# Layer 0 of a spectral attention kernel: where the next image batch's sums, loads and spectra stand, and what GpSimd does behind attention's products

## The chip, the cores and the metric

One core of a Trainium2 chip. The time is the device time of one execution of the program in microseconds (us); below, the median of several executions. A profiled execution gives the trace: what each engine did at each moment. Engines are named as the profile names them: PE is the matmul engine and PEld its weight loads, DVE is VectorE, ACT is ScalarE, POOL is GpSimd, SP is the queue of SyncE that issues transfers.

## The reference, cut to what matters

The input x has shape (4, 32, 128, 128): 4 batches of 32 images. Layer 0 normalises x by groups, runs a spectral attention block on each batch and adds it to x; layer 1 (token attention and experts) follows and isn't touched by the change.

```python
x = x + _L0_conv_ref(_gn(x), ...)
# within _L0_conv_ref, for each batch:
xn = _inorm(xa, norm1_w, norm1_b)              # every image to mean 0, variance 1
k, q, v = (_fno_layer(xn, ...) for K, Q, V)    # spectral convolutions to 32 heads
scores = einsum('bntk,bnsk->bnts', qf, kf) / sqrt(Hs * Ws)   # image against image, per head
p_attn = softmax(scores);  av = einsum('bnts,bnsk->bntk', p_attn, vf)
p = _fno_layer(av, Pcw, Psw, H, W)
a = _inorm(p + xa, attn_w, attn_b);  an = _inorm(a, norm2_w, norm2_b)
m = _fno_layer(an, m0cw, m0sw, H, W, inner_norm=True, act=True)    # gelu
m = _fno_layer(m, m1cw, m1sw, H, W, inner_norm=True, act=False)
out = _inorm(m, mon_w, mon_b) + a
```

## The kernel before, in words

Everything is computed in frequency space. Layer 0 is a Python loop `for b in range(B)` (line 702) over the four batches. The trace calls a batch's 32 images together "image b" below. What b + 1 needs at its start is prepared inside the body of b. In program order, a pass of the loop is:

- `load(b + 1)` (lines 122 to 127, called at 707): four transfers of 512 KB, two on SP's queue and two on ACT's, into the second of two x buffers.
- The head weights: `cm` (718), `cd` (720), `cp` (721), `bd` (726), which are made of the attention weights `ph` and needed by the skip products `sk` (757).
- The value loop over `x0` in five steps of four (766 to 803): a broadcast of the spectra (`xb`, 773, on SP), a copy to PSUM (`xw`, ACT, 782), products with the value weights (`u`, 788 on POOL, 790 on DVE), and matmuls into `po` (793) with the weights `pr`.
- Back to images (813, `inverse` at 267), statistics, the first spectra of q (`spectra(0, q)`, 937), the chain of scale factors `v0`, `r0`, `hq`, `hs0`, `hb` (938 to 949), then `back` (288) with the gelu (956 to 966).
- `logarithms()` (972) puts the logarithm table back on ACT; `image_sums(b + 1)` (320 to 393, called at 974): squares of x (326), matmuls that sum rows (330), then a chain of small operations on DVE with two inverse deviations, each a logarithm and an exponential on ACT (`inv_std`, 203).
- `stats("gl")`, `spectra(1, gl)` (982), `spectra_of_images(b + 1)` (418 to 459, called at 984), and the second scale chain `v1`, `vc`, `r1`, `rm`, `c2`, `cq` (985 to 1007).
- `attention_weights(b + 1)` (489 to 595, called at 1009). It copies rows to PSUM (`xp`, 501), and for each of 17 column frequencies `yy` makes two products, `pa` on DVE (534) and `pb` on POOL for even `yy` and on DVE for odd (533 to 536), which PE multiplies into `sp` (540, 542). Then come `spt` (544), the logits `sc` in two halves one after the other (549 to 558), softmax (562 to 579), and two transfers by way of HBM that give `pr` (587, 592).
- The end (1010 to 1031): ACT scales g (1014), POOL adds it to the residue in four pieces (`xr`, 1021), `back` runs again and DVE adds its result (1025), and SP stores x1 (1031).

The order of instructions on each engine isn't written out: within layer 0 the framework's scheduler orders them at build time. What is earlier in the program has priority, and what is ready and finds its buffer free can be taken ahead of its place. Buffers are shared by tag. In PSUM the tags "wide" (two buffers of two banks), "a" and "b" (two of one bank each) take all eight banks: `rows8`, `s12` and the small sums of `image_sums` are "wide", and so are `xp`, `so`, `sc`, `y1` of `back`, and `xw`. In SBUF the tag "pr" has six buffers, shared by the squares, `u`, `sod`, `pa`, `pb`, `spt`, `ex` and `ph`; "pk" and "pk_sq" have one each, shared by `image_sums` and `stats`. Layer 1 has an order written out by hand and starts when layer 0 is done with PE.

Of the kernel before, what the change touches and what calls it, by code (L numbers as in the profile page):

```python
# [7 lines left out]
F32 = mybir.dt.float32  # L8
AF = mybir.ActivationFunctionType
ALU = mybir.AluOpType  # L10
# [98 lines left out]
def layer0(  # L109
# [11 lines left out]

    def load(b):
        xt = images.tile([P, T, C], F32, name=f"x_{b}", tag="x")
        for g in range(0, T, GI):
            eng = nc.sync if g % 16 == 0 else nc.scalar
            eng.dma_start(out=xt[:, g : g + GI], in_=x[b, g : g + GI].rearrange("t w c -> w t c"))
        return xt
# [50 lines left out]
    grp, small = (p.__enter__() for p in work)  # L178
    pools += work

    flip = [0]
# [70 lines left out]

    def forward(images, c1, c2, take, change):


        n = c1.shape[1]
        z = grp.tile([P, GI, 192], F32, name="z", tag="z")
        first_step(images, z)
        change(z)
        for k in range(0, GI, 4):  # L260
            px = ps.tile([P, 4, n], F32, name="px", tag="b")
            for j in range(4):
                nc.tensor.matmul(px[:, j], z[:, k + j, :P], c1, start=True, stop=False)
                nc.tensor.matmul(px[:, j], z[:, k + j, 64:], c2, start=False, stop=True)
            take(k, px)
# [44 lines left out]

    def sums(name, matrix, src):

        m = ps.tile(list(src.shape), F32, name=name, tag="wide")
        nc.tensor.matmul(m, matrix, src, start=True, stop=True)
        return m

    def one(name, n=1):
        return small.tile([P, n], F32, name=name, tag=name)

    def image_sums(b, xt):  # L320


        rows8 = ps.tile([64, 4, C], F32, name="rows8", tag="wide")
        for g in GROUPS:
# [13 lines left out]
        nc.scalar.copy(ev, rows8)  # L338
        s12 = ps.tile([P, 2, 512], F32, name="s12", tag="wide")[:, :, :T]
        for j in range(4):  # L340
            for k in range(2):
                r = slice(32 * k, 32 * k + 8)
                nc.tensor.matmul(s12[:, k, j::4], ev[r, j], ident[r, r], start=True, stop=True)
        sv = small.tile([P, 2, T], F32, name="sv", tag="pk_sq")
        nc.vector.tensor_copy(sv, s12)

        tot = one("tot", 2)
        nc.vector.tensor_reduce(tot, sv, AX.X, ALU.add)
        mg = sums("mg", group, tot)
        gm = one("gm")  # L350
# [11 lines left out]
        by_group = small.tile([P, 2, 32], F32, name="by_group", tag="by_group")  # L362
        nc.vector.tensor_copy(by_group, sums("bg", ones, both))
        n = 1 + 2 * KY
        colg = small.tile([P, 2, n], F32, name="colg", tag="colg")
        nc.vector.tensor_scalar(colg[:, 0], cols1[:, :n], gr, None, ALU.mult)
        nc.vector.tensor_scalar(colg[:, 1], cols2[:, :n], gr, None, ALU.mult)
        m128 = one("m128")
        nc.vector.tensor_scalar(m128, gm, 128.0, None, ALU.mult)

# [14 lines left out]
        nc.vector.tensor_scalar(y12, y12, 1.0 / NPIX, None, ALU.mult)  # L385
        my = sums("my", ones, y12)
        ym, yv = per_image("ym"), per_image("yv")
# [4 lines left out]
        ysc = scalars(ALU.mult, "n1_s", yr, par[:, N1W : N1W + 1])  # L392
        return by_group, colg, m128, ysc

# [23 lines left out]
    def spectra_of_images(b, xt, normed):  # L418


        _, colg, m128, ysc = normed
        n = 1 + 2 * KY
        xx = modes.tile([P, T, n], F32, name=f"xx_{b}", tag="xx")
        xd = dram.tile([T, 2, KX, KY], F32, name=f"xd_{b}")
        for g in GROUPS:

# [5 lines left out]

            def less_mean(z):
                nc.vector.tensor_scalar(z[:, :, 0], z[:, :, 0], m128, None, ALU.subtract)
                nc.vector.tensor_scalar(z[:, :, P], z[:, :, P], m128, None, ALU.add)

            forward([xt[:, g + t] for t in range(GI)], colg[:, 0], colg[:, 1], scaled, less_mean)

# [49 lines left out]

    def attention_weights(b, front):

# [36 lines left out]
        for yy in range(KA):  # L527
# [3 lines left out]
            for k, t in enumerate((pa, pb)):  # L531
                other = (xm[:, yy] if k else xe[:, yy, :T]).unsqueeze(2).to_broadcast(tt)
                if k == 0 or yy % 2 == 1:
                    nc.vector.tensor_tensor(t, steps(row, [1, T], [1, nd]), other, ALU.mult)
                else:
                    nc.gpsimd.tensor_tensor(t, steps(xe[:, yy], [1, T], [1, nd]), other, ALU.mult)
            turn = dict(start=yy < 2, stop=yy >= KA - 2)
# [10 lines left out]
        sc = ps.tile(nn, F32, name="sc", tag="wide")  # L548
        for h in range(2):
            i = slice(half * h, half * h + half)  # L550
            o = sc[32 * h : 32 * h + 32]
            nc.tensor.matmul(o, qk, sod[:, i], start=True, stop=False)
            nc.tensor.matmul(o[:, :, 1:nd], both_plus, spt[:, 0, i], start=False, stop=False)
            first = spt.rearrange("p r t d -> p (r t d)")[:, (half * h + nd) * half + half - 2 :]
            nc.tensor.matmul(
                o[:, :, nd:], plus_minus, steps(first, [half, half], [half - 1, half - 1]), start=False, stop=False
            )
            nc.tensor.matmul(o[:, :, 0], both_plus[: 2 * NH], spt0[:, i], start=False, stop=True)


# [22 lines left out]
        for k in range(2):  # L583
# [10 lines left out]
            )  # L594
        return ph, pr

# [50 lines left out]
    big, late = (p.__enter__() for p in (pools[-1], right[-1]))  # L647
    weights = attention_weights(0, front)

# [42 lines left out]

    pv = const.tile([2 * NH, 1], F32, name="pv")
    nc.sync.dma_start(out=pv[:NH], in_=heads[:, 2:3])
    nc.sync.dma_start(out=pv[NH:], in_=heads[:, 2:3])
    psw2 = const.tile([2 * NH, 1], F32, name="psw2")
    nc.sync.dma_start(out=psw2[:NH], in_=heads[:, 3:4])
    nc.sync.dma_start(out=psw2[NH:], in_=heads[:, 3:4])
    nc.vector.tensor_mul(pv, pv, psw2)


    for b in range(B):
        xt = loaded
        by_group, _, _, ysc = normed
        xd = front[2]
        if b + 1 < B:
            loaded = load(b + 1)

        ph, pr = weights

        cp = per_image("cp")
        sel = scalars(ALU.mult, "sel", same, ysc)
        for h in range(2):
            r = slice(32 * h, 32 * h + 32)
            cm = ps.tile([P, T, 16], F32, name="cm", tag="a")
            nc.tensor.matmul(cm, pv[r].to_broadcast([NH, P]), ph[r], start=True, stop=True)
            cd = grp.tile([P, T, 16], F32, name="cd", tag="v", bufs=3)
            nc.vector.tensor_tensor(cd, cm, sel.unsqueeze(2).to_broadcast([P, T, 16]), ALU.mult)  # L720
            nc.vector.tensor_reduce(
                cp[:, 16 * h : 16 * h + 16], cd.rearrange("p s t -> p t s"), AX.X, ALU.add
            )
        nc.vector.tensor_add(cp, cp, same)
        bd = small.tile([P, 4, T], F32, name="bd", tag="bd")
        nc.vector.tensor_tensor(
            bd,
            block.unsqueeze(2).to_broadcast([P, 4, T]),
            cp.unsqueeze(1).to_broadcast([P, 4, T]),
            ALU.mult,  # L730
        )
        q = big.tile([P, T, C], F32, name=f"q_{b}", tag="q")
# [33 lines left out]
        for x0 in range(0, KX, NK):  # L766
# [3 lines left out]
            for i in range(4):  # L770
                xb = late.tile([P, 2, NK * KY], F32, name="xb", tag="xb")[:, :, :m]
                for r in range(2):
                    nc.sync.dma_start(
                        out=xb[:, r],
                        in_=xd[8 * i : 8 * i + 8, r, x0 : x0 + nk]
                        .rearrange("s x y -> s (x y)")
                        .unsqueeze(1)
                        .to_broadcast([8, 16, m]),
                    )
# [20 lines left out]
                if i % 2 and at_c < C:  # L800
                    skips(at_c)
                    at_c += 16
            nc.scalar.copy(rs[:, x0 : x0 + nk].rearrange("p x y -> p (x y)"), po)
        if b + 1 == B:
            for p in reversed(right):
                p.__exit__(None, None, None)
# [141 lines left out]
        nc.vector.tensor_mul(dq, dq, hs0)  # L948
        nc.vector.tensor_tensor(hb, hb, dq, ALU.add)
        gl = big.tile([P, T, C], F32, name=f"g_{b}", tag="y")  # L950
        st = grp.tile([P, T, 6], F32, name="st", tag="st")
# [20 lines left out]
        logarithms()  # L972
        if b + 1 < B:
            normed = image_sums(b + 1, loaded)
        else:
            first((ps, images))
# [5 lines left out]
        spec, sq = spectra(1, gl)  # L982
        if b + 1 < B:
            front = spectra_of_images(b + 1, loaded, normed)
        v1 = weighed("v1", sq, squares, layers[1][2])
# [22 lines left out]
        if b + 1 < B:  # L1008
            weights = attention_weights(b + 1, front)
        for a in HALVES:  # L1010
            groups = [slice(16 * a + g, 16 * a + g + GI) for g in (0, GI)]
            for i in groups:
                for t in range(i.start, i.stop):
# [6 lines left out]
                    )  # L1020
                nc.gpsimd.tensor_tensor(xr[:, i], xr[:, i], gl[:, i], ALU.add)

# [638 lines left out]
```

## Time and profile before

| what | value |
|---|---|
| median of 3 runs | 3184.4 us (3181.8 to 3186.39) |
| the profiled execution, its own time | 3176.48 us |
| its span, first to last instruction | 3174.4 us |
| busy share of the span: PE, DVE, ACT, POOL | 92%, 71%, 73%, 65% |
| mean granted PE clock | 0.954 |
| first `po` matmul of images 0, 1, 2, 3 | 107.33, 362.84, 623.00, 882.33 us |
| first matmul of layer 1's attention (1461) | about 1088 us |

Two successive images are 255 to 260 us apart. The profile's page lists busy time by engine, the chain of waits that ended last, and groups of instructions by line; the trace gives each instruction's start, its duration, and, where its engine had been idle, for how long and what ended that. "PEclk" is the granted share of PE's full clock.

### The profile page before, as it was taken

The page shows a single profiled execution, that of the slowest core. Times are in us where ns is not written, and L with a number is a line of the kernel's source. Part 1 is how long each engine was busy: PE and PEld are TensorE (multiplying, and loading weights), DVE is VectorE, ACT ScalarE, POOL GpSimd, SP SyncE. Part 2 cuts the span into 40 slices and gives each one's busy share as a digit, 9 for nine tenths or more (in the row PEclk, how much of TensorE's full clock was granted, in tenths as well). Part 3 has the DMA queues.
Part 4 walks back from the last instruction along what each step waited for, and adds up shares of the span by engine and source line. Part 5 has one row for each costly group of instructions (what it writes and reads, how often), then busy time and mean ns, then how long its engine had stood idle before and what let it go on. Part 6 is the DMA issues. An engine that isn't in the chain of part 4 may idle for free.

```text
span 3174.4 us, 52863 instructions
## 1 busy us (share of the span) xinstructions
PE 2911.8 (92%) x19530; PEld 1437.6 (45%) x19530; DVE 2257.4 (71%) x5054; ACT 2318.2 (73%) x3142; POOL 2053.0 (65%) x1819
## 2 busy tenths in 40 slices
PE   7888889798888789999999999999999999999997
PEld 4366366355446444444344444443444444444443
DVE  5776676667578557777666868866778776777887
ACT  2444343354354589998999999998999999999992
POOL 1621440350270388878888797889878889888773
PEclk8898898799798799999999999999999999999998
DMA  6401310220130201010111010021010011101000
GB/s 139 120 10 30 107 39 22 72 82 1 38 124 1 66 23 31 9 29 7 31 37 24 14 24 14 7 46 29 17 37 1 14 37 24 37 1 31 14 14 14
DMA packets 152306, 112.74 MB, mean 36 GB/s; under 512 B 36878, under 2 KB 140657, under 8 KB 151441
## 3 DMA queue, kind: packets, MB, share of 16 engines
q1 hardware_dynamic: 136209, 103.61, 12.3%
q10 hardware_dynamic: 15840, 5.77, 0.8%
q8 instruction: 154, 2.52, 0.3%
q14 instruction: 103, 0.84, 0.1%
HBM read 68.37 MB, written 20.00 MB: 28 GB/s over the span
## 4 chain that ended last, share of the span: by engine, by line
PE 62%; POOL 12%; ACT 9%; DVE 8%; issue 6%; DMA 2%; SPq 0%; POOLq 0%; DVEq 0%; ACTq 0%
PE d L1461 19%; PE po L1480 11%; PE px L1367 6%; ACT r L1511 5%; PE po L793 4%; PE n L1461 3%; POOL e L1520 3%; POOL e L1519 3%; PE pz L248 2%; PE four L308 2%; ACT e L1527 2%; PE px L886 2%; POOL kx L1126 1%; PE sk L757 1%; DVE r L1516 1%
## 5 line engine op out<-in xcount | busy, mean ns | idle before, releaser
L1516 DVE TENSOR_TENSOR r<-n,r 128x1024 f32<-128x1024 f32 (+1 forms) x1056 | 962.0, 953 | 478.3 <-PE n L1461 393.4
L1519 POOL TENSOR_TENSOR e<-r 128x512 f32<-128x512 f32 x528 | 673.0, 1275 | 268.7 <-DVE r L1516 268.1
L1511 ACT ACTIVATE r<-d 128x1024 f32<-128x1024 f32 (+1 forms) x1056 | 792.8, 802 | 68.8 <-PE n L1461 59.0
L1523 ACT ACTIVATE r<-r 128x1536 f32<-128x1536 f32 x528 | 783.6, 1484 | 16.8
L1520 POOL TENSOR_TENSOR e<-e,r 128x512 f32<-128x512 f32 x528 | 671.2, 1271 | 41.4
L1461 PE MATMUL d<-qe,ke 32*128 32x512 f32 (+3 forms) x2304 | 606.3, 602 | 39.8 <-ACT r L1511 36.5
L1480 PE MATMUL po<-e,kx 128*128 128x512 f32 (+3 forms) x1152 | 594.5, 605 | 15.7 <-POOL e L1532 15.7
L1461 PE MATMUL n<-qe,ke 32*128 32x512 f32 (+3 forms) x2304 | 606.7, 602 | 0.0
L1461 PE MATMUL n<-qf,kf 32*128 32x512 f32 (+3 forms) x2304 | 552.7, 554 | 0.0
L1461 PE MATMUL d<-qf,kf 32*128 32x512 f32 (+3 forms) x2304 | 550.3, 553 | 0.0
L1371 DVE SCALAR_TENSOR_TENSOR xc<-px,wgt,xc 128x128 f32<-128x128 f32 x1024 | 358.4, 351 | 43.0 <-PE px L1367 10.5
L1527 ACT ACTIVATE e<-e 128x512 f32<-128x512 f32 x528 | 325.8, 617 | 65.9 <-POOL e L1520 65.1
L1480 PEld LDWEIGHTS po<-e,kx 128*128 128x128 f32 x1152 | 175.5, 188 | 393.0 <-issue 308.5
L1461 PEld LDWEIGHTS d<-qe,ke 32*128 32x128 f32 x2304 | 176.5, 183 | 359.6 <-ACT r L1511 339.8
L788 POOL TENSOR_TENSOR u<-xb,gb 128x858 f32<-128x858 f32 (+1 forms) x120 | 233.5, 1968 | 156.6 <-PE po L793 110.4
L1461 PEld LDWEIGHTS d<-qf,kf 32*128 32x128 f32 x2304 | 220.4, 186 | 176.2 <-issue 164.1
L1367 PE MATMUL px<-we,x2t 128*128 128x512 f32 x512 | 265.9, 605 | 6.9 <-DVE xc L1371 5.9
L790 DVE TENSOR_TENSOR u<-xw,gb 128x858 f32<-128x858 f32 (+1 forms) x200 | 206.9, 1086 | 58.3 <-PE po L793 51.8
L1461 PEld LDWEIGHTS n<-qf,kf 32*128 32x128 f32 x2304 | 228.7, 185 | 18.9 <-issue 11.1
L900 POOL TENSOR_TENSOR spec<-part,part 128x512 f32<-128x512 f32 x16 | 24.8, 1552 | 323.7 <-DVE part L897 80.3
L793 PE MATMUL po<-u,pr 128*32 128x429 f32 (+1 forms) x1280 | 194.0, 551 | 26.3 <-DVE u L790 14.4
L1461 PEld LDWEIGHTS n<-qe,ke 32*128 32x128 f32 x2304 | 177.8, 183 | 9.2 <-DVE r L1516 0.8
(395 smaller groups left out, 3760.5 us busy)
## 6 DMA issues: line engine op xcount, KB each, us to landing
xb<-xd SPq DMA_DIRECT2D x128, 214.5 KB
xc<-x SPq DMA_DIRECT2D x29, 512.0 KB
x<-x SPq DMA_DIRECT2D x16, 512.0 KB
qf<-qe SPq DMA_DIRECT2D x64, 128.0 KB
out<-xc SPq DMA_DIRECT2D x15, 512.0 KB
xb<-xd SPq DMA_DIRECT2D x32, 198.0 KB
gb<-gd SPq DMA_DIRECT2D x4, 1056.0 KB
x<-in_x SPq DMA_DIRECT2D x8, 512.0 KB
```

The lines of the kernel that those rows point to most:

```text
L788: nc.gpsimd.tensor_tensor(u, xb, gk, ALU.mult)
L793: nc.tensor.matmul(po[32 * j : 32 * j + 32], pr[:, i, k], u[:, r], start=i == 0 and k == 0, stop=i == 3 and k == 1,)
L1367: nc.tensor.matmul(px, x2t[:, k * P : (k + 1) * P], we[:, e0 : e0 + 4], start=True, stop=True)
L1371: nc.vector.scalar_tensor_tensor(xc[:, k], px[:, e], wgt[:, k, e0 + e : e0 + e + 1], xc[:, k], ALU.mult, ALU.add)
L1461: nc.tensor.matmul(o, k, q, start=turn == 0 or g > 0, stop=turn == 1 or g > 0)
L1480: nc.tensor.matmul(sums[c, h][:, q0 : q0 + c1 - c0], kx[:, jb], e[:, c0:c1], start=jb == 0, stop=is_last and q0 > 2 * P, skip_group_check= ...
L1511: nc.scalar.activation(r[:, g], d, AF.Ln, scale=1.0 / DSCALE)
L1516: nc.vector.tensor_tensor(r[:, g], part, r[:, g], ALU.mult)
L1519: nc.gpsimd.tensor_tensor(e, r[:, 1], r[:, 2], ALU.add)
L1520: nc.gpsimd.tensor_tensor(e, e, r[:, 0], ALU.add)
L1523: nc.scalar.activation(r, r, AF.Exp, scale=-1.0)
L1527: nc.scalar.activation(e, e, AF.Exp)
```

## The change

It touches layer 0 alone, in these places:

1. **Products.** `pb` goes to DVE where `yy % 3 == 2` (5 of 17) and to POOL otherwise (12 of 17); before, 8 and 9. The four POOL additions of line 1021 get an order edge behind the last POOL product.
2. **Logits.** The two halves of `sc` are issued in turn, matmul by matmul, instead of one half after the other.
3. **Head weights.** `cm`, `cd`, `cp`, `bd` move from the head of the pass into the end of `attention_weights`, ahead of the second `back`.
4. **Image sums.** `image_sums(b + 1)` moves from behind the gelu to ahead of it; its PSUM tiles go from "wide" to "a" and "b".
5. **Spectra.** In `spectra_of_images` the first step of group g + 1 is issued ahead of the second step of group g; the mean's removal is one DVE addition instead of two operations. The whole function moves behind the second scale chain.
6. **Loads.** `load(b + 1)` moves into the value loop, after its second `x0` step, all four transfers on SP with an order edge behind that step's last broadcast. The loads of `pv` and `psw2` in the prologue come before the first `attention_weights`.

```diff
@@ load
-            eng = nc.sync if g % 16 == 0 else nc.scalar
+            eng = nc.sync if behind is not None or g % 16 == 0 else nc.scalar
...
+            if behind is not None:
+                tc.add_manual_dep(d.ins, behind.ins.name, ...NoSync..., reason="order")
@@ image_sums
-        rows8 = ps.tile([64, 4, C], F32, name="rows8", tag="wide")
+        rows8 = ps.tile([64, 4, C], F32, name="rows8", tag="a")
...
-        s12 = ps.tile([P, 2, 512], F32, name="s12", tag="wide")[:, :, :T]
+        s12 = [ps.tile([P, T], F32, name=f"s{t}", tag=t) for t in "ab"]
...
-        mg = sums("mg", group, tot)
+        mg = sums("mg", group, tot, "a")
@@ spectra_of_images
-        for g in GROUPS:
+        steps = []
+        for g in (*GROUPS, None):
+            if g is not None:
+                z = grp.tile([P, GI, 192], F32, name="z", tag="z")
+                first_step([xt[:, g + t] for t in range(GI)], z)
+                nc.vector.tensor_tensor(
+                    z[:, :, ::P], z[:, :, ::P], shift.unsqueeze(1).to_broadcast([P, GI, 2]), ALU.add
+                )
+                steps.append((g, z))
+                if g == 0:
+                    continue
+            g, z = steps.pop(0)
...
-            def less_mean(z):
-                nc.vector.tensor_scalar(z[:, :, 0], z[:, :, 0], m128, None, ALU.subtract)
-                nc.vector.tensor_scalar(z[:, :, P], z[:, :, P], m128, None, ALU.add)
@@ attention_weights
-                if k == 0 or yy % 2 == 1:
+                if k == 0 or yy % 3 == 2:
...
-                    nc.gpsimd.tensor_tensor(t, steps(xe[:, yy], [1, T], [1, nd]), other, ALU.mult)
+                    last_product = nc.gpsimd.tensor_tensor(t, steps(xe[:, yy], [1, T], [1, nd]), other, ALU.mult)
...
-        for h in range(2):
-            i = slice(half * h, half * h + half)
-            o = sc[32 * h : 32 * h + 32]
+        halves = [(sc[32 * h : 32 * h + 32], slice(half * h, half * h + half)) for h in range(2)]
+        for o, i in halves:
             nc.tensor.matmul(o, qk, sod[:, i], start=True, stop=False)
+        for o, i in halves:
             nc.tensor.matmul(o[:, :, 1:nd], both_plus, spt[:, 0, i], start=False, stop=False)
...
-        return ph, pr
+        cp = per_image("cp")
+        sel = scalars(ALU.mult, "sel", same, ysc)
...
+        return pr, bd, last_product
@@ loop over b
-        if b + 1 < B:
-            loaded = load(b + 1)
...
             nc.scalar.copy(rs[:, x0 : x0 + nk].rearrange("p x y -> p (x y)"), po)
+            if x0 == NK and b + 1 < B:
+                loaded = load(b + 1, broadcast)
...
         nc.vector.tensor_tensor(hb, hb, dq, ALU.add)
+        if b + 1 < B:
+            normed = image_sums(b + 1, loaded)
...
         logarithms()
-        if b + 1 < B:
-            normed = image_sums(b + 1, loaded)
-        else:
+        if b + 1 == B:
             first((ps, images))
...
         spec, sq = spectra(1, gl)
-        if b + 1 < B:
-            front = spectra_of_images(b + 1, loaded, normed)
...
         if b + 1 < B:
-            weights = attention_weights(b + 1, front)
+            front = spectra_of_images(b + 1, loaded, normed)
+            weights = attention_weights(b + 1, front, normed[3])
...
-                nc.gpsimd.tensor_tensor(xr[:, i], xr[:, i], gl[:, i], ALU.add)
+                added = nc.gpsimd.tensor_tensor(xr[:, i], xr[:, i], gl[:, i], ALU.add)
+                if b + 1 < B:
+                    behind(added, weights[2])
```

## The prediction, made before the result was known

> **What bounds the kernel now.** I read the page first. The profiled execution took 3176.5 us, its span 3174.4. In its 40 slices PE is at 9 tenths from the sixteenth on (layer 1 begins at 1088 us), and before that between 7 and 9 tenths, at a clock of 7 to 9 tenths. The change touches only the first third, so I cut one period of that, from image 1's value loop to image 2's, into stages and asked for busy times and clock in each.
>
> ```profile
> core 0: us, PE busy (x) PEld busy (x) DVE busy (x) ACT busy (x) POOL busy (x), PEclk, DMA share, GB/s
> 362.80:431.40 68.60, 65.21 (x640) 30.20 (x640) 50.38 (x51) 38.53 (x84) 54.09 (x28) 0.96 0.45 134
> 431.40:471.50 40.10, 38.56 (x430) 34.17 (x430) 27.39 (x94) 12.86 (x24) 1.27 (x1) 0.96 0.01 2
> 471.50:484.00 12.50, 4.71 (x66) 4.35 (x66) 11.67 (x39) 1.45 (x4) 2.17 (x1) 0.58 0.00 1
> 484.00:504.90 20.90, 20.87 (x114) 9.59 (x116) 16.97 (x66) 18.17 (x40) 0.00 (x0) 0.93 0.00 1
> 504.90:556.00 51.10, 47.02 (x389) 38.78 (x385) 28.82 (x113) 12.84 (x31) 2.53 (x2) 0.93 0.14 35
> 556.00:588.70 32.70, 22.75 (x138) 8.74 (x138) 19.55 (x40) 15.45 (x36) 19.33 (x13) 0.75 0.08 19
> 588.70:623.00 34.30, 26.34 (x163) 12.46 (x162) 19.51 (x49) 6.82 (x11) 3.99 (x2) 0.76 0.23 58
> ```
>
> The stages are: value loop, back to images and first spectra, scale chain, gelu, sums and spectra, products, logits to the next value loop. The first two are PE's. Over the last five PE is idle for 30 of 151 us, at low clock in three of them. Those are what the change is about, at three boundaries (0-1, 1-2, 2-3).
>
> The chain of waits names who ends the product stage:
>
> ```profile
> 565.07 1.13 POOL pb L536
> 566.20 2.32 POOL x L1021
> 568.52 1.09 POOL pb L536
> 569.66 1.10 PE sp L540 x6
> ```
>
> POOL alternates product and addition, and PE waits for the product. The timelines of PE and DVE give the other places (in brackets: idle time before, and what ended it):
>
> ```profile
> 477.76 0.64 PE L314 MATMUL ms<-v_s,ones 128*128 128x32 f32 x2 [6.33 <-DVE v_s L930]
> 502.13 0.62 PE L330 MATMUL rows<-xx,one_of 128*32 128x512 f32 x1
> 548.46 1.03 PE L263 MATMUL px<-colg,z 128*128 128x67 f32 x4 [1.41 <-DVE v L993]
> 591.34 1.04 PE L552 MATMUL sc<-sod,qk 32*32 32x512 f32 x2
> ...
> 620.08 1.91 DVE L721 TENSOR_REDUCE cp<-cd 128x16 f32<-128x512 f32 x2
> 621.91 1.04 DVE L790 TENSOR_TENSOR u<-xw,gb 128x858 f32<-128x858 f32 x1
> ```
>
> PE idles 6.33 us in the scale chain, and does the row sums later, among and after the gelu's matmuls; the second half of the logits starts only when the first is done; and the head weights' reduction is the last thing ahead of the next image's first `u`.
>
> **Products (saves 9 us a boundary).** From the end of `sod` to `spt` is 561.1 to 588.75, 27.7 us. The prologue does the same products without additions in 23.1 (64.1 to 87.2). So the four additions (2.36 each, 9.4) cost only 4.6 of their length; the rest is a loop: in the prologue one pair of frequencies takes 2.31 us, in which POOL works 1.13 and waits 1.18 for PE to hand back a "pr" buffer. After the change DVE makes 22 products, back to back at 0.635 us (trace: 74.03, 74.66), 14.0 us, and POOL 12 at 1.13, 13.6. Per three frequencies that is 2.54 on DVE against 2.26 on POOL. `sod` holds one of six "pr" buffers until both first logits matmuls are done; now both can run at 561, which gives that buffer back. I take 1.0 us a frequency, 17, plus 1.5 for the start: 18.5, so 9. Bounds: 4.6 (the loop's pace stays) to 12 (14.0 + 1.5). The additions land behind the last product, from about 576 to 586; nobody needs them until the second `back`'s first DVE addition (603.82 now), so they are hidden; if POOL were late by all of it, up to 9.4 would come back. Queued behind them is `u` of line 788, which then waits for `po` anyway (23.0 us).
>
> Here a rule speaks against the change. The Trainium skill, "SBUF — State Buffer", section "Who interferes with whom": a DVE instruction with two SBUF inputs and a POOL instruction that reads SBUF lock each other out for a whole instruction. The trace agrees: a DVE multiplication of 32 columns (line 211) took 0.83 us, not 0.19, while POOL's addition of 900 ran (466.12 to 467.39). By the rule the moved additions can block `ph` (line 574, two SBUF inputs) for up to 2.36 us, on the path. The products escape, as their row operand is in PSUM: line 534 has 702, 715, 726 ns as minimum, median and maximum beside a busy POOL. By my times the additions end before `ph` begins (about 588), so I book 0 of 2.36.
>
> **Logits (2.2).** Line 552 to 558 of the second half run 591.34 to 593.89, 2.55 us, on `mx`'s path. The halves write different 32-row strips, and `rows8`'s two strips show such matmuls running together (500.11 and 500.12, each 0.59). I take 2.2; bounds 1.5 and 2.5. The prologue has it too.
>
> **Head weights (1).** `cd` and `cp` are 1.28 + 1.91 us of DVE. Moved ahead they leave the end (1.91 saved there) and enter a stretch where DVE waits for PE in pieces of 0.3 to 1.9 us. Net 1.0; bounds 0 and 2.
>
> **Image sums, spectra, second chain (6).** The row sums are 8.2 us of PE (1.0, 1.9, 5.3 in three pieces), and fit the 6.33 gap but for 2. PE's later stages lose them. PE's clock is the second gain: `four` at 484.0 took 3.48 for four records, 1.98 at full clock: 1.5 us. Third, the first step one group ahead removes waits for evacuation (1.32, 1.41, 0.53 us). Against this: the sums' chain is 34 DVE operations, at some 0.14 us from start to start (514.67 to 515.20: 5 of them) 4.8 us, that now fall beside the gelu, where DVE is busy 17.0 and ACT 18.2 of 20.9 us. And its two logarithm-exponential pairs may land after the gelu's table is in; the table load is 1.28 us (485.12), so a pair inside costs two, 2.6 us. In favour: `stats("gl")` no longer queues behind the sums for "pk_sq" and "pk" (its matmul now waits until 521.0, 16 us after the last gelu). Moving the second chain ahead of the spectra hands its 12 us of DVE to PE as first steps to run beside. Sum: 8.2 + 1.5 + 1.6 (half of 3.3) - 4.8 (DVE, uncovered in the gelu) - 1.3 (half of a pair's loads) = 5.2; I take 6, for the statistics that no longer queue. Bounds: -4 and +13 (all of 8.2, 1.5 and 3.3 without the costs).
>
> A second rule bears on the third item. The skill, "TensorE: Matmul & The Clock Gate", section "HAM oscillation — how this bites in real kernels", says that PE idle gaps of more than about 3.4 us drop the clock to half. In 2-us rows the clock falls from 1.00 to 0.86 and 0.50 after 471.5, as it says. But it also falls to 0.63 and 0.50 at 548, after a gap of 1.41 us, and stays there until 565. By the rule removing such small gaps is worth their 3.3 us; by the row another 4 (the 8 us of matmuls from 548 to 556 at half clock). I count none of the 4, since the next stage's waits would lower the clock anyway.
>
> **Loads (1 each for three images; prologue 3).** SP loses two issues (1.25 us at 625.18) ahead of `xb`, and 2 MB of x no longer compete with image b's first broadcasts (`xb` is on the chain for 9.67 us at 626.79). But the loops of images 1, 2 and 3 last 68.6, 67.5 and 67.8 us, and image 3 loads only half as much, so the collision is nearly hidden: 1; bounds 0 and 3. In their new place the four issues stand ahead of `xb` on SP, 2 us, covered by `xb`'s four buffers; without that cover as much returns. In the prologue `ex` stands on ACT behind `xw`, which waits for `xb` until 96.7; products and logits gain 6.8 there, but only what `xb` comes earlier counts. I take 3; bounds 0 and 8.
>
> **Sum.** 9 + 2.2 + 1 + 6 = 18.2 per boundary, times three 54.6; loads 3, prologue 3: 60.6, say 60. The profiled 3176.5 would become 3116.5; the median of the runs is 7.9 above it, so 3124. What is late next: in the products DVE, then the second `back`, which waits for "wide" buffers.
>
> **Rivals.** Measurement tells 0.2%, 6 us, from no change.
> - *The sums don't pay.* Their DVE operations and table loads in the gelu eat what PE gains, and DVE or ACT becomes the bound there: -4 instead of +6. For: ACT's 18.2 of 20.9. Against: PE has no gap at all in that stage. 3124 + 30 = 3154.
> - *It doesn't do what it says.* The scheduler orders by its own estimate; PE's next wait (for "wide", for `xb`, for DVE's 1025) ends at the same time. For: `back` waits for PSUM. Against: the chain runs through POOL. 3182.
> - *Slower.* The logarithms and exponentials of image b + 1 are scattered among the gelus, each with its own change of table: up to eight loads, 10.3 us, and the sums' chain waits on them and holds an "a" buffer meanwhile, so that the first steps that need both stand for up to another 6 (the gap that PE has now). The point from which it decides is a loss of 14.2 us a boundary (12.2 from the other parts and 2 from loads and prologue). For: the chain's data are ready only near 484. Against: DVE would have to wait for ACT each time. At 16 lost: 3184 + 3 x 1.8 = 3190.
>
> **How the numbers follow.** The forecast's own case 0.60 (3095 to 3145); sums don't pay 0.31 (3140 to 3168); no effect 0.04; slower 0.05. All high bounds together would give 3 x 29.5 + 9 + 8, a time of 3079; all low ones (4.6 + 1.5 - 4, three times) 3178. The range that leaves out 2 in 10 is 3095 to 3162. Faster 0.91, same 0.04, slower 0.05.
>
> **What would show it.** Products: `sod` to `spt` near 18.5 us, POOL's products close together, additions behind them. Logits: `spt` to `mx` near 2.5 us instead of 5. Sums: row sums inside 471 to 484 as measured from the scale chain, no idle gap of 6 us, clock 1.00 in the gelu; table loads per boundary still two. `cp` ahead of 1025. Value loops of 66 to 67 us. It is wrong if the stage from gelu to `so` keeps its 51 us, or the second `back` gets longer by what the products lose.

## The result, and the profile after

The median of four runs of the changed kernel is 3143.8 us (3142.2 to 3144.0), against 3183.1 (3169.4 to 3186.4) of four runs of the kernel before beside it: a ratio of 0.989, interval 0.986 to 0.992. The forecast was 3124, within 3095 to 3162. The profiled execution after took 3144.0 us with a span of 3142.3, clock 0.956; before it was 3174.4. So the two traces differ by 32.1 us, where the forecast said 60.6. Both traces are cut at the same events:

| stage, from one event to the next | before | after | difference | forecast |
|---|---|---|---|---|
| start to the first `po` | 107.3 | 109.3 | +2.0 | -3 |
| value loops of images 0, 1, 2 (first `po` to first `py`) | 203.7 | 216.9 | +13.2 | -3 |
| three times first `py` to first gelu | 167.7 | 185.0 | +17.3 | |
| three times gelu | 54.6 | 63.8 | +9.2 | |
| three times last gelu to `so` | 152.0 | 110.2 | -41.8 | |
| the last three together | 374.3 | 359.0 | -15.3 | -18 |
| three times `so` to `spt` | 96.9 | 65.9 | -31.0 | -27 |
| three times `spt` to `mx` | 15.5 | 8.1 | -7.4 | -6.6 |
| three times `mx` to the next `po` | 84.6 | 96.4 | +11.8 | -3 |
| last image, to layer 1 | 206.1 | 202.0 | -4.1 | 0 |
| layer 1 | 2086.0 | 2084.7 | -1.3 | 0 |

Products, logits and sums came as forecast or near it. Loads, the way from `mx` to `po` (where the head weights were booked), and the start came with the opposite sign. The stages of the changed kernel's trace that answer to those shown of before (value loop of image 1; back to images and first spectra; scale chain; gelu; sums and spectra; products; logits to the next value loop):

```profile
core 0: us, PE busy (x) PEld busy (x) DVE busy (x) ACT busy (x) POOL busy (x), PEclk, DMA share, GB/s
357.40:430.30 72.90, 64.86 (x641) 30.38 (x641) 50.55 (x49) 38.69 (x84) 54.24 (x28) 0.95 0.44 137
430.30:478.00 47.70, 46.01 (x464) 37.80 (x464) 35.03 (x112) 13.80 (x25) 3.45 (x2) 0.96 0.01 1
478.00:490.60 12.60, 9.54 (x90) 6.68 (x90) 8.69 (x55) 4.31 (x11) 0.00 (x0) 0.66 0.01 2
490.60:509.40 18.80, 17.21 (x122) 11.06 (x120) 16.95 (x71) 16.30 (x38) 0.00 (x0) 0.96 0.00 1
509.40:550.20 40.80, 37.11 (x323) 34.10 (x323) 22.87 (x81) 11.66 (x27) 3.45 (x2) 0.87 0.13 27
550.20:573.60 23.40, 22.10 (x140) 10.79 (x142) 16.30 (x29) 14.68 (x35) 14.53 (x13) 0.85 0.19 53
573.60:606.40 32.80, 24.39 (x164) 11.38 (x167) 23.22 (x46) 6.92 (x11) 12.75 (x6) 0.77 0.22 54
```

In the products PE now works 22.1 of 23.4 us, where it worked 22.75 of 32.7. In the value loop it does the same work as before (64.9 us of it) in 72.9 us instead of 68.6. The lines of POOL and PE that answer to those shown of before, from their timelines:

```profile
321.60 2.22 POOL L560 TENSOR_TENSOR pb<-xe,xm 128x544 f32<-128x544 f32 x2 [0.30 <-DVE pa L558]
323.78 4.67 POOL L1043 TENSOR_TENSOR x<-x,g 128x1024 f32<-128x1024 f32 x2
...
475.85 0.59 PE L345 MATMUL rows<-x,one_of 128*32 128x512 f32 x1
476.82 0.41 PE L329 MATMUL ms<-v_s,ones 128*128 128x32 f32 x2 [0.38 <-DVE v_s L953]
```

POOL's additions (line 1043) follow its last product (line 560), and the products wait for DVE, which forms three `pa` and one `pb` in 2.52 us without a pause. The row sums fill the gap ahead of `ms`: 6.33 us of idle time have become 0.38.

### The profile page after: what moved, and what is told of

The parts are those of the page before. It is cut to its first block, busy times and chain, and to the rows that moved or that the text cites. A ratio compares the mean times of both kernels' runs of the same rounds, so it can differ in the third digit from the quotient of the medians.

```text
span 3142.3 us, 52841 instructions
## 1 busy us (share of the span) xinstructions
PE 2889.5 (92%) x19530; PEld 1450.8 (46%) x19530; DVE 2253.9 (72%) x5034; ACT 2326.2 (74%) x3150; POOL 2070.7 (66%) x1831
## 3 DMA queue, kind: packets, MB, share of 16 engines
q10 hardware_dynamic: 9600, 2.62, 0.4%
q8 instruction: 154, 2.52, 0.3%
## 4 chain that ended last, share of the span: by engine, by line
PE 61%; POOL 10%; ACT 10%; DVE 9%; issue 6%; DMA 2%; SPq 1%; POOLq 0%; DVEq 0%; ACTq 0%
PE d L1485 19%; PE po L1504 11%; PE px L1391 6%; ACT r L1535 4%; PE po L814 4%; PE n L1485 4%; POOL e L1544 3%; POOL e L1543 3%; PE pz L266 2%; PE four L323 2%; ACT e L1551 2%; POOL kx L1150 1%; PE sk L778 1%; PE sp L564 1%; DVE r L1540 1%
## 5 line engine op out<-in xcount | busy, mean ns | idle before, releaser
L1547 ACT ACTIVATE r<-r 128x1536 f32<-128x1536 f32 x528 | 783.6, 1484 | 16.8
L1551 ACT ACTIVATE e<-e 128x512 f32<-128x512 f32 x528 | 325.7, 617 | 65.4 <-POOL e L1544 64.6
L811 DVE TENSOR_TENSOR u<-xw,gb 128x858 f32<-128x858 f32 (+1 forms) x200 | 207.0, 1089 | 70.9 <-PE po L814 49.2
L1485 PEld LDWEIGHTS n<-qf,kf 32*128 32x128 f32 x2304 | 229.4, 186 | 20.5 <-issue 13.2
## 6 DMA issues: line engine op xcount, KB each, us to landing
xb<-xd SPq DMA_DIRECT2D x128, 214.5 KB
```

What stands on the lines that cost most here:

```text
L1485: nc.tensor.matmul(o, k, q, start=turn == 0 or g > 0, stop=turn == 1 or g > 0)
L1547: nc.scalar.activation(r, r, AF.Exp, scale=-1.0)
L1551: nc.scalar.activation(e, e, AF.Exp)
```

## The experiments

**How they are measured.** Each kernel is the changed one with one edit (two in tags_back, xb_early and late_psum). Its ratio is to runs of the kernel before on the same chip. The groups ran on different chips, on which the kernel before took 3173.5 to 3183.1 us, so the ratios are compared, and the stages of each trace. 0.001 is 3.2 us. "loops", "so-spt" and the like are sums over three images or boundaries, as in the table of stages; "first po" is a time.

| kernel | ratio, interval | loops | py-so | so-spt | mx-po | first po |
|---|---|---|---|---|---|---|
| changed, first group | 0.989 (0.986 to 0.992) | 216.9 | 359.0 | 65.9 | 96.4 | 109.3 |
| changed, again | 0.9907 (0.9891 to 0.9922) | 215.1 | 359.3 | 65.9 | 96.2 | 111.3 |
| loads_back | 0.9917 (0.9903 to 0.9931) | 210.1 | 365.5 | 72.8 | 96.8 | 108.6 |
| loads_late | 0.9880 (0.9866 to 0.9893) | 199.5 | 359.5 | 68.1 | 96.6 | 111.5 |
| sm_psum | 0.9881 (0.9864 to 0.9899) | 214.7 | 359.2 | 72.4 | 80.6 | 110.5 |
| edge_off | 0.9929 (0.9913 to 0.9945) | 215.3 | 357.8 | 86.7 | 78.3 | 109.2 |
| tags_back | 0.9934 (0.9918 to 0.9950) | 214.8 | 367.0 | 63.6 | 95.8 | 111.4 |
| tags_wide | 0.9994 (0.9982 to 1.0005) | 214.5 | 387.8 | 70.9 | 93.3 | 109.5 |
| sums_pow | 0.9956 (0.9942 to 0.9969) | 214.8 | 377.4 | 66.9 | 96.2 | 110.8 |
| sums_one | 0.9902 (0.9886 to 0.9919) | 215.3 | 358.2 | 71.7 | 95.4 | 108.1 |
| pv_early | 0.9914 (0.9901 to 0.9928) | 211.9 | 357.4 | 74.1 | 94.7 | 109.3 |
| xb_early | 0.9925 (0.9909 to 0.9940) | 214.5 | 358.4 | 65.8 | 96.0 | 116.9 |
| late_psum | 0.9817 (0.9803 to 0.9830) | 199.7 | 360.5 | 68.4 | 81.9 | 111.1 |

The product stage differs from the changed kernel's by up to 8 us in kernels that don't touch it: POOL's first products catch or miss a buffer (16.2 or 18.4 us from `sod` to `spt` in one trace), and an edit elsewhere can tip that. So a ratio alone is not a verdict on 3 us; the stage that the edit touches is.

> The changed kernel itself once more, so that the others of this group have it beside them on the same chip. Nothing else than 0.989 of before is expected, by every theory, and the same stages within 1 us up to the second image.

It came out alike: 0.9907, and no summed stage differs by more than 2 us. The first `po` comes 1.9 us later and image 0's loop is 2.0 us shorter, where 1 was expected.

### Where the loads stand

The changed kernel in its second `x0` step, on SP, ACT and PE in turn (in brackets the idle time before, and what ended it):

```profile
368.78 0.57 SPq L794 DMA_DIRECT2D xb<-xd  x1
369.40 7.39 SPq L126 DMA_DIRECT2D x<-in_x  x4
376.90 11.18 SPq L794 DMA_DIRECT2D xb<-xd  x10
...
383.93 0.52 ACT L803 COPY xw<-xb 128x429 f32<-128x429 f32 x1 [5.94 <-DMA xb<-xd]
...
387.22 1.64 PE L814 MATMUL po<-u,pr 128*32 128x429 f32 x2 [3.69 <-ACT rs L824]
```

The four issues take SP 7.39 us, unevenly (the third alone 4.05); the next broadcast leaves behind them, ACT stands 5.94 us for it, and PE in turn. Before, with SP idle for 1.7 us ahead of its two issues:

```profile
620.81 2.67 SPq L773 DMA_DIRECT2D xb<-xd  x2
625.18 1.25 SPq L126 DMA_DIRECT2D x<-in_x  x2
```

Two kernels put the load elsewhere.

```diff
 loads_back:
         pr, bd, _ = weights
+        if b + 1 < B:
+            loaded = load(b + 1)
...
-            if x0 == NK and b + 1 < B:
-                loaded = load(b + 1, broadcast)
 loads_late:
-            if x0 == NK and b + 1 < B:
+            if x0 + NK >= KX and b + 1 < B:
```

> The load of the next image goes back to the head of the loop, two transfers on SP and two on ACT; all else is as after. Theory (the four issues of 1.85 us each on SP, amid the value loop, hold up the broadcasts xb behind them, and 2 MB of x share the DMA engines with them): the loops of images 0, 1 and 2 go back from 72 us to about 67.6, nothing else moves, 3144 becomes about 3131. Rival (the loops grew by something else, such as u on DVE or the lower clock): they stay at 72, and the time is the same within 3 us or a little longer.

Measured: loops of 67.7, 72.2 and 70.2 us, 0.9917. Image 0's loop is back where it was, the others only partly: my theory, that the old place is free of cost, falls. What differs from before is that the loops now begin sooner: SP is done with the stores of x1 at 356.2 us and the first `po` comes at 356.7, where before it was 359.3 and 362.8. So `xb` has 3 us less lead when 2 MB of x join the queue, and the first broadcast behind them takes SP 4.15 us to issue (362.78), where most take 0.57. That this is the whole reason was not tried.

> The load of the next image is issued behind the last broadcast of the value loop instead of behind the second. Theory: no broadcast is left that the four issues could hold up, so the loops of images 0 to 2 take 66 to 68 us and the time is 3128 to 3132. Rival (the loops grew by something else): 72 us and 3144. A third possibility: x now lands too late for the next image's sums, which would show as a longer scale chain.

Measured: 67.0, 66.3 and 66.2 us, 0.9880, and the sums' stages stay (359.5). Behind the last broadcast the load hinders nobody, and x still comes in time. In one row, for image 1's loop:

```profile
core 0: us, PE busy (x) PEld busy (x) DVE busy (x) ACT busy (x) POOL busy (x), PEclk, DMA share, GB/s
355.20:421.50 66.30, 62.13 (x642) 29.69 (x642) 50.76 (x49) 38.73 (x84) 54.64 (x28) 1.00 0.49 151
```

The DMA share is no lower than in the changed kernel (0.49 against 0.44): the loop moves the same bytes, and what counts is where x stands among the broadcasts. Whether these were held by SP's long issues or by sharing the DMA engines with x (busy to 0.80 from 369.3 to 383.0 in the changed kernel) these runs don't separate. PE's clock is 1.00, and with it PE's own work is 2.7 us less. Over three images the load inside the loop costs 15 to 17 us by the loops; by the spans of loads_late and the changed kernel run again it is 12.7, by their ratios 0.0027, 9 us.

### The additions behind the products, and `ph`

```diff
 sm_psum:
-        sm = small.tile([2 * NH, half], F32, name="sm", tag="mx")
+        sm = ps.tile([2 * NH, half], F32, name="sm", tag="a")
```

> The tile sm (the reciprocal of the softmax sums) lies in PSUM instead of SBUF, so that the product ph on DVE has one SBUF input instead of two; the work and nearly all of the order are the same. Theory (DVE and POOL lock each other out at SBUF when both inputs of a DVE product lie there): ph goes from 5.30 to about 2.1 us in the three boundaries, 3.2 us each, and the time from 3144 to about 3134. Rival (ph is long for another reason, say its input ex): ph stays at 5.3 and the time is the same.

Measured: 0.9881, and `ph` as the theory had it. DVE and POOL at boundary 1-2, first in the changed kernel:

```profile
572.41 9.28 POOL L1043 TENSOR_TENSOR x<-x,g 128x1024 f32<-128x1024 f32 x4
...
579.88 5.30 DVE L600 TENSOR_TENSOR ph<-ex,sm 32x512 f32<-32x512 f32 x2
```

and with `sm` in PSUM:

```profile
571.39 9.28 POOL L1043 TENSOR_TENSOR x<-x,g 128x1024 f32<-128x1024 f32 x4
...
578.88 2.16 DVE L600 TENSOR_TENSOR ph<-ex,sm 32x512 f32<-32x512 f32 x2
```

The two operations overlap in time alike; only where one operand lies differs, and 3.14 us go. Before, with both inputs in SBUF but no addition beside it, `ph` was as short:

```profile
597.44 2.14 DVE L574 TENSOR_TENSOR ph<-ex,sm 32x512 f32<-32x512 f32 x2
```

That is the lock which the Trainium skill states ("SBUF — State Buffer", section "Who interferes with whom"), now shown here.

The way from `mx` to `po` fell by more, 15.6 us in three boundaries, and 8.4 of it at the last (36.5 to 28.1). The order of instructions in that stretch is the same, the clock isn't. The changed kernel from `mx` to `po`, in four pieces (columns as above):

```profile
819.00:828.00 9.00, 4.78 (x46) 2.86 (x46) 7.62 (x7) 1.06 (x1) 8.06 (x4) 0.74 0.08 7
828.00:840.00 12.00, 11.21 (x42) 5.64 (x44) 8.05 (x20) 1.19 (x2) 2.00 (x1) 0.50 0.13 16
840.00:848.00 8.00, 7.64 (x51) 5.61 (x50) 2.17 (x6) 1.09 (x3) 0.00 (x0) 0.50 0.35 103
848.00:855.60 7.60, 5.18 (x8) 1.30 (x7) 5.39 (x18) 2.49 (x5) 0.00 (x0) 0.83 0.16 50
```

and with `sm` in PSUM, in three:

```profile
817.40:825.00 7.60, 5.53 (x50) 3.87 (x51) 5.16 (x8) 1.06 (x1) 7.60 (x5) 0.77 0.17 16
825.00:837.00 12.00, 10.53 (x61) 5.83 (x61) 8.41 (x23) 1.19 (x2) 1.70 (x1) 0.72 0.08 12
837.00:845.50 8.50, 5.23 (x36) 2.20 (x36) 6.33 (x20) 3.58 (x7) 0.00 (x0) 1.00 0.49 145
```

PE waits 3.13 us for the locked `ph` (at 825.30), then works 19 of 20 us at clock 0.50, until 848. Without the lock it waits 1.57 us, falls to 0.50 as well, but is back at 0.80 by 832. Why the low clock lasts so much longer in one case is open.

```diff
 edge_off:
-                added = nc.gpsimd.tensor_tensor(xr[:, i], xr[:, i], gl[:, i], ALU.add)
-                if b + 1 < B:
-                    behind(added, weights[2])
+                nc.gpsimd.tensor_tensor(xr[:, i], xr[:, i], gl[:, i], ALU.add)
```

> The four additions on POOL lose their order edge and stand among the products again, as before the change; the split of 12 and 5 products stays. Theory (the edge is worth what the additions cost amid the products, less what they cost behind them): so to spt goes from 21 to 23 us to 25 to 28, ph back from 5.3 to 2.1, so some 1 to 3 us a boundary are lost, 3 to 9 in all, about 3151. Rival (with 12 products POOL has room for the additions, and all that the edge brings is the locked ph): so to spt stays at 21 to 23, ph is 2.1, and the time falls by 8 to 10 us to about 3136.

Measured: so-spt 86.7 instead of 65.9, mx-po 78.3 instead of 96.2, `ph` 2.1 us, 0.9929. The edge gave 6.9 us a boundary to the products and took 6.0 back behind them: alone it is worth about 1 us a boundary, less than what the product stage differs by from kernel to kernel. The other 3.4 us a boundary by which the products are shorter than before (96.9 to 86.7) are there without it. The theory holds in kind; the products alone came out longer than the 25 to 28 us expected (26.0, 31.0 and 29.7).

### The sums ahead of the gelu

In tags_wide the tiles `rows8`, `s12`, `mg`, `bg` and `my` are "wide" again; tags_back has that and the place behind the gelu.

```diff
 tags_wide and tags_back:
-        rows8 = ps.tile([64, 4, C], F32, name="rows8", tag="a")
+        rows8 = ps.tile([64, 4, C], F32, name="rows8", tag="wide")
...
 tags_back:
-        if b + 1 < B:
-            normed = image_sums(b + 1, loaded)
...
         logarithms()
+        if b + 1 < B:
+            normed = image_sums(b + 1, loaded)
```

> Part 4 undone: image_sums stands behind the gelu again, and its PSUM tiles are wide again; spectra and second chain stay as changed. Theory (the sums ahead of the gelu are what shortens the stage from gelu to so, at the price of the stages ahead of them): back to images, scale chain and gelu take 75 us together instead of 80 to 85, the gelu needs two table loads, gelu to so takes some 50 us instead of 37, and the time is 12 to 18 us longer, about 3159. Rival (the gain of that stretch is owed to the spectra one group ahead and the second chain, and the sums' move only shifts time from one stage to the other): from py to so the sum of the stages is the same within 3 us a boundary, and the time stays at 3144.

Measured: py-so 367.0, which is 7.7 above the changed kernel's (359.3) and 7.3 below before's (374.3); 0.9934. So the two halves of the gain are equal: 7.7 us from the sums' new place with its tags, 7.3 from spectra and second chain. My theory had the direction and put it at 12 to 18.

> Only the PSUM tags of the sums go back to wide; image_sums stays ahead of the gelu in the program. Theory (the row sums start early because they no longer wait for a wide buffer, so the tags and not the place do it): the row sums run at the gelu's end as before, and the stages and the time are those of the kernel with the whole part undone, within 4 us. Rival (the place in the program does it): row sums early as in the changed kernel, gelu 22 us, and 3144.

Measured: neither. 0.9994, the time of before. The row sums stand ahead of the gelu, but not in the gap. Image 1 in this kernel, on PE:

```profile
483.89 0.64 PE L329 MATMUL ms<-v_s,ones 128*128 128x32 f32 x2 [6.33 <-DVE v_s L954]
484.45 1.06 PE L345 MATMUL rows<-x,one_of 128*32 128x512 f32 x1
```

The gap of 6.33 us stays, the row sums follow it, at first at half clock (1.06 us each instead of 0.59), with their whole chain ahead of the gelu: py to gelu is 220.8 us for three images, against 185.0. The new place pays only with the narrow tags, with which the row sums stand ahead of `ms`; that they do so because they need no wide buffer is likely, not shown. The narrow tags at the old place were not run.

In the gelus of images 0 and 2 the changed kernel loads ACT's table four more times each than before. ACT, image 2:

```profile
741.92 1.28 ACT L226 ACT_TABLE_LOAD   x1
743.22 0.23 ACT L226 ACTIVATE n_r<-n_r_ve 128x32 f32<-128x32 f32 x1
743.46 1.28 ACT L984 ACT_TABLE_LOAD   x1
744.76 0.49 ACT L984 ACTIVATE g<-g,hb,hs 128x128 f32<-128x128 f32 x1
745.27 1.28 ACT L227 ACT_TABLE_LOAD   x1
746.57 0.23 ACT L227 ACTIVATE n_r<-n_r 128x32 f32<-128x32 f32 x1
746.81 1.28 ACT L984 ACT_TABLE_LOAD   x1
```

Two kernels take the logarithm and exponential of the sums away: sums_pow takes a power on POOL instead, sums_one leaves them out and starts the Newton step from 1.

```diff
 sums_pow, in inv_std for the sums:
-        nc.scalar.activation(r, ve, AF.Ln)
-        nc.scalar.activation(r, r, AF.Exp, scale=-0.5)
+        nc.gpsimd.tensor_tensor(r, ve, nhalf0.to_broadcast([P, n]), ALU.pow)
 sums_one:
+        nc.vector.tensor_scalar(r, ve, 0.0, 1.0, ALU.mult, ALU.add)
```

> The two inverse deviations of the next image's sums are taken with a power on POOL (and the same Newton step on DVE) instead of a logarithm and an exponential on ACT, so that they need no table. Theory (the gelu stages of images 0 and 2 last 22.5 us because of four table loads and two pairs among the gelus): no more than two loads a boundary, the gelu of images 0 and 2 takes 18 to 19 us, image 1's stays, and the time falls by 7 to 9 us to about 3136. Rival (DVE with the sums' chain bounds the gelu, and ACT's loads lie in its gaps): the gelus keep 22 us and the time stays within 3 us.

Measured: ten table loads, as before, and 0.9956: 16 us slower. The new cost hid the old one. POOL and DVE, image 2:

```profile
745.64 5.43 POOL L229 TENSOR_TENSOR n_r<-n_r_ve,nhalf 128x32 f32<-128x32 f32 x1 [7.60 <-DVE n_r_ve L227]
...
751.10 0.19 DVE L233 TENSOR_TENSOR n_r_t<-n_r 128x32 f32<-128x32 f32 x1 [5.29 <-POOL n_r L229]
```

The power of 32 columns takes 5.43 us on POOL; the Newton step waits for it at the head of DVE's order, with the gelu's inputs behind it. It is no test of the table loads.

> In the next image's sums the two inverse deviations start their Newton step from 1, set by one small DVE operation, instead of from a logarithm and an exponential on ACT: the logarithm and the exponential are left out, all else is there. The run with the power on POOL did not answer the question, since the power of 128 by 32 took 4.4 to 5.4 us there and DVE stood behind it. Theory (the table loads in the gelus of images 0 and 2, 5.1 us of ACT each, and DVE's wait for them are what makes those gelus 22.5 us): two loads a boundary, the gelus of images 0 and 2 at 17.5 to 19 us, and 7 to 9 us off the time, about 3137. Rival (the scheduler's other order and DVE's sums bound the gelu): gelus of 21 us or more, or what they lose comes back as waits for so, and the time stays within 3 us of 3146.

Measured: ten table loads, gelus of 19.3, 19.0 and 16.8 us, 8.7 less than the changed kernel's 63.8. But the last gelu to `so` takes 118.3 us instead of 110.4, so py-so is nearly the same (358.2), and so is the time (0.9902): the rival, in its second form. The two stages of image 2 show how, first in the changed kernel (run again), then here:

```profile
741.80:764.20 22.40, 17.78 (x152) 12.20 (x144) 17.99 (x68) 21.55 (x44) 0.00 (x0) 0.92 0.00 1
764.20:795.50 31.30, 29.75 (x292) 27.30 (x291) 21.56 (x79) 11.56 (x27) 3.45 (x2) 1.00 0.17 36
```

```profile
735.90:752.70 16.80, 11.55 (x100) 7.17 (x100) 15.69 (x66) 15.18 (x38) 0.00 (x0) 1.00 0.00 1
752.70:793.90 41.20, 39.11 (x343) 33.37 (x344) 22.96 (x81) 12.90 (x28) 3.45 (x2) 0.92 0.13 27
```

While ACT loads tables, PE does some fifty matmuls of the next stage (152 against 100 in the gelu, 292 against 343 behind it). In sum the 10.2 us of table loads in two images cost the whole about 1. By image it isn't even: from the first gelu to `so`, image 2 is 4.3 us longer without them (58.0 against 53.7), and image 0 is 5.2 us shorter (55.7 against 60.9). PE's clock moves as well (0.92 and 1.00 against 1.00 and 0.92 in the rows of image 2). So it is shown that taking the loads away brings nothing in sum, not that PE covers them in every image.

### The start

In pv_early the loads of `pv` and `psw2` and their product move to the head of the prologue, on ACT's queue. In xb_early, besides, the loads of the masks (`mcw`, `mcol`, `mrow`) and what is made of them become a function that the loop of image 0 calls.

```diff
 pv_early and xb_early, for pv and psw2:
-    nc.sync.dma_start(out=pv[:NH], in_=heads[:, 2:3])
+    nc.scalar.dma_start(out=pv[:NH], in_=heads[:, 2:3])
...
 xb_early, in the value loop:
+            if x0 == NK and b == 0:
+                mask_columns()
```

In the changed kernel the product of `pv` and `psw2` stands among the first image's products, and waits for a transfer that SP issues at 76.7 us, behind the stores of xd:

```profile
82.05 0.15 DVE L699 TENSOR_TENSOR pv<-pv,psw 64x1 f32<-64x1 f32 x1 [13.13 <-DMA psw<-in_heads]
```

> The loads of pv and psw2 and their product are issued with the other head parameters at the start, on ACT's queue. Theory (the multiplication stands in DVE's order amid the first image's products and waits 13 us for a transfer that SP issues late): the gap at 82 us goes, and the first po comes at 97 to 100 us instead of 109, which gives 3132 to 3135. Rival (the first po is bound by the broadcasts xb on SP, whatever DVE does): the products end earlier, but po moves by less than 3 us and the time is the same.

Measured: the gap is gone, the first image's products last from 70.8 to 87.8 us instead of 63.0 to 91.6 (they begin later because `so` does; why is open), and the first `po` comes at 109.3 as it did: the rival. ACT in that kernel:

```profile
94.06 0.52 ACT L803 COPY xw<-xb 128x429 f32<-128x429 f32 x1 [1.48 <-DMA xb<-xd]
94.52 1.00 ACT L575 COPY spt<-sp 128x1024 f32<-128x1024 f32 x1
```

`spt` has its input at 89.1 and is copied at 94.5: it stands behind `xw`, which waits for `xb`.

> pv and psw2 are loaded at the start on ACT's queue, and the sixteen small loads of the masks (16 issues on SP, 8 us, ahead of the first broadcasts) move behind the second step of the first value loop. Moving pv and psw2 alone had taken the 13 us gap out of the products, and the first po stayed at 109 us: ACT copies xw ahead of spt, and xw waits for xb, which SP issues at 88. Theory (the first po is bound by xb on SP): xb is issued at about 80 us, spt is copied at about 89 instead of 94.5, and the first po comes at 101 to 105 us: 5 to 8 us off the time. Rival (xd's stores, which end at 80, and their landing bound xb, or the chain of softmax and ph does): the first po moves by less than 3 us.

Measured: `xb` is issued at 80.4 and `spt` copied at 90.0, as the theory said, and the first `po` comes at 116.9, later. DVE in that kernel:

```profile
98.75 0.20 DVE L718 TENSOR_SCALAR turned<-mrow 128x64 f32<-128x64 f32 x1 [10.56 <-DMA mrow<-in_mrows]
```

A product of the masks has moved ahead of `mx` in DVE's order and waits for its own load. Three times in this prologue one small operation that waits for a transfer holds a whole engine; a version without any such wait was not run, so what the start could give is open.

### Both mends together

> Both mends together: the next image's load behind the last broadcast of the value loop, and sm in PSUM. Theory (the two costs lie in different stages and are independent): loops of images 0 to 2 at 66 to 67 us, ph at 2.1 us, the way from mx to the third boundary's po at some 28 us instead of 36.6; against before 0.984 to 0.986, some 22 us less than the changed kernel. Rival (one wait covers the other, such as the broadcasts xb that the earlier ph then waits for): no better than the better one alone, 0.988.

Measured: 0.9817 (0.9803 to 0.9830), a median of 3119.5 us against 3176.9; loops of 68.0, 66.3 and 65.4, `ph` 2.1, the third boundary 28.0 us. Each cost stands for itself: 0.0090 below the changed kernel's 0.9907 is 28.6 us by the ratios, 24.7 by the spans (3144.1 and 3119.4), a little more than the 22 expected; by the spans the two mends alone give 12.7 and 12.4.

## Why the prediction came out half right

The sign held and the time lies in the stated range; the size did not hold: 39 us by the medians, where 60 was said. The measured 3143.8 lies where the forecast's own case (to 3145) and its rival "the sums don't pay" (from 3140) overlap, so the time alone tells neither. The stages do: the sums paid, and the loss lay in two steps that were booked as a gain or at nothing. By its own steps:

- **Products** (-9 a boundary; -10.3). The pace of DVE, 2.52 us for three frequencies, is what was worked out. `sod` to `spt` was 16.2, 18.4 and 16.2 us where 18.5 was said. What failed stands in the same step: "By my times the additions end before `ph` begins (about 588), so I book 0 of 2.36." Counted from the end of `sod` (561.1), these times are the additions from 15 to 25 us and `ph` at 27: before's 36.3 less the 9 of the products. The 2.2 us that the logits save came in the next step and were not taken off `ph`; with them it falls at 24.7, and no margin is left. Measured: `ph` at 22.5, 24.7 and 22.5 us, the additions from 15.0, 17.2 and 15.0 to 24.3, 26.5 and 24.3. So they met at every boundary. It cost 3.14 us each, more than the 2.36 that were weighed, since both operations of `ph` were held (2.65 and 2.62 us instead of 1.05); what sm_psum took off this stretch beyond that went with a higher clock.
- **Logits** (-2.2; -2.5). Right: `spt` to `mx` is 2.7 us.
- **Head weights** (-1; +3.9 a boundary). The step counted the head weights alone, but this stretch carries the locked `ph` too. Where `ph` is free (sm_psum, edge_off, late_psum) it is 78.3 to 81.9 us for three, 1 to 2 less a boundary than before: the forecast's size.
- **Image sums, spectra, second chain** (-6 a boundary; -5.1). The sum is near, and its halves were 2.6 for the sums and 2.4 for the rest. The 6.33 gap is filled, as said. The table loads came as the rivals had them, four more in each of images 0 and 2, but taking them away (sums_one) brought nothing in sum. The gelu's clock is 0.92, 0.96 and 0.92, not 1.00: the clock still falls to 0.50 from 482 to 490, with waits of 0.42 and 1.97 us about it; in the products it is 0.85 where it was 0.75.
- **Loads** (-1 each; +4.4 each). The failing step is "the four issues stand ahead of `xb` on SP, 2 us, covered by `xb`'s four buffers; without that cover as much returns". The issues took 7.39 us: I took the price of two issues after idle time (1.25 us) for four of 512 KB right behind broadcasts. The cover did not hold either: ACT stood 5.94 us for `xb`.
- **Prologue** (-3; +2.0). Counted was "only what `xb` comes earlier". It did come earlier: ACT's first copy of it (`xw`) stands at 91.71 us instead of 95.82. What failed is the order behind it: before, only `ex` stood behind `xw` on ACT (97.20); now `spt` does (93.86), with `mx` and `ex` still to come, and `ph` starts at 101.03 instead of 99.27. The product of `pv`, in DVE's order ahead of its data, delayed `spt`; without that (pv_early) `spt` is copied behind `xw` all the same, at 94.52.
- **Not forecast**: the last image is 4.1 us shorter in this pair of traces. Over the kernels above, whose edits don't touch it, it is 199.9 to 205.4, so much of this may be spread; before's 206.1, from one trace, lies just outside, so that isn't shown.

Loads and `ph` are the miss: +16.2 and +14.8 us against their forecasts, together a little more than the 28.5 by which the traces miss it. With both mended the kernel comes to 0.9817, and before's 3184.4 times that is 3126, about the forecast time; the start is still late in it (111.1), so that this fits so well is partly luck.

## What to carry to other kernels

A step that is made faster pulls forward what follows it; place every later step at its new time before asking whom it meets. Large loads on a queue that also feeds the running loop belong behind the loop's last transfer, and their issue time has to be read from such a moment, not from an idle queue. Before paying to remove a busy stretch on one engine, look at what the bounding engine does meanwhile: eight table loads less brought about 1 us in sum, one wait put at the head of DVE's order cost 16.

## What was not expected of the hardware

- Four DMA issues of 512 KB right behind broadcasts held SP for 7.39 us; two after 1.7 us of idle time took 1.25.
- Two DVE operations of 32 by 512 took 5.30 us beside POOL's additions with both inputs in SBUF, 2.16 with one of them in PSUM.
- POOL's power took 5.4 us for 128 by 32 values and 0.56 for 128 by 1.
- PE stayed at clock 0.50 for 20 us while it worked 19 of them (828 to 848 in the changed kernel).
